# A three-pass transformer block on one core: one gate product fewer, another order of the drain of the second pass, and a weight sum ahead of the keys

## The chip, the core and the metric

The kernel runs on one core of a Trainium2 chip. A core has TensorE (matmuls, PE in the profile; its weight loads are PEld), VectorE (DVE), ScalarE (ACT), GpSimd (POOL) and SyncE (SP), which here only issues DMAs. Each engine takes its own list of instructions in order; engines wait for each other and for DMAs on semaphores. Matmuls read SBUF and write PSUM, and another engine has to empty PSUM. The metric is the device time of one execution in microseconds; lower is better. The time of a kernel is the median of several runs.

## The reference, cut to what matters

Inputs are 4 x 1024 tokens of 1024 numbers, in float32. The block is "macaron" shaped: half a feed-forward, attention, and half of the same feed-forward again.

```python
def ffn(x):                        # weight (1024,1024), centroids (64,1024)
    dots = softmax(x @ centroids.T / 0.1)
    hits = dots > 0.01
    query_sel = any(hits, axis=1)  # one flag per token
    cluster_sel = any(hits, axis=0)            # one flag per cluster, over ALL tokens
    row_sel = cluster_sel[assignments]         # one flag per output column
    dense = x @ weight.T + bias
    return where(query_sel[:, None] & row_sel[None, :], dense, 0)

def attn(x):                       # 32 query heads of 32, 8 key/value heads
    q, k, v = x @ Wq + bq, x @ Wk + bk, x @ Wv + bv
    scores = einsum('bsdh,bseh->bsde', q, k) / sqrt(32)    # 32 x 32 for every token
    return einsum('bsde,bseh->bsdh', softmax(scores), v)

x = x + 0.5 * ffn(layernorm(x))
x = x + attn(layernorm(x))
x = x + 0.5 * ffn(layernorm(x))
```

The attention mixes within one token, so there is no dependence between tokens there. The feed-forward has one: `cluster_sel` needs the gate of every token before the first output can be masked.

## The kernel before

The tokens are 32 tiles of 128. Because of `cluster_sel` there are three passes. The first makes the dense product and the gate of the first feed-forward. The second adds it, does the attention, and makes the gate (and the last 256 dense columns) of the second feed-forward. The third makes the remaining dense product, adds, and stores the result.

Everything stands in an order written by hand: the tile framework's manual schedule keeps the instructions on each engine's list as the Python code issues them, and derives only the semaphores. Generators are used for this: `next(steps)`, `next(two)`, `next(sums)` issue the next piece of a longer computation at that place of the list.

Products of two tiles with the 768 first columns are made by Strassen's method in Winograd's form: `winograd` (L258) makes seven products of quarter size in place of eight, numbered 1, 5, 2, 6, 7, 3, 4 in the order of issue. It needs four sums of activations s1 to s4 (`token_sums`, L242) and four sums of weights t1 to t4 (`weight_sums`, L233); both run on GpSimd. t1 uses the weight blocks w12 and w11; t2 uses w22 and t1; t3 uses w22 and w12; t4 uses w21 and t2. `project_two` (L785) is the same for the projection to queries, keys and values, with sums `qsums` of the projection's weights, which are kept in the place of the feed-forward's weight blocks during the second pass. The feed-forward's blocks wait in DRAM (`wtd`) and are loaded again (`returns`, L985) before the drain; the sums t1 to t4 then take the place of the projection's weights.

The second pass is the loop at L990 over s = 0 to 36. Step s is a software pipeline: it projects tile s, makes the keys of s-1 (`keys`, GpSimd, L857), scores and softmax of b = s-2 (`scores`, `weighted`, `attend`: matmuls `sc` at L880, VectorE's maximum L889 and subtraction L891, ScalarE's exp L1000, VectorE's transpose `stt` L900, matmuls `po` L922, four VectorE steps L932/L934 to `o`), the residual add of g = s-3 (`second_added`, GpSimd, L946), its layernorm (`moments` on VectorE with the square root on ScalarE, `normed` on ScalarE), the transposes of f = s-4 (`transposed`, matmuls `tp` L205 and ScalarE copies L206), and the gate products of a = s-5 or f (`gate_2`, L974: `ffn_part`, eight matmuls of 320 columns, then VectorE's evacuation L222, maximum L388, subtraction L391, ScalarE's exp L397 and VectorE's bookkeeping L403 to L409 in `gates_used`). `scores` and `attend` use the same PSUM buffer (tag `att`, one buffer).

The projected tile goes to DRAM and back to be regrouped (`rearranged`, L844: one load `qk`, four loads `v`), and so does the attention's result (`od`, `ot`). All these DMAs stand on SP's queue, in program order; the stores of `store_2` (L966) and of y stand on GpSimd's.

From s = 32 on, nothing is projected any more: this is the drain. Its TensorE cover is the dense product of the last six tiles (26 to 31, called kept), by `winograd` over pairs. Its weight sums are issued at L1102 to L1104 (the first ahead of s1, the second by the `between` of `token_sums`, L253, between s2 and s3) and at L1067 to L1069. The gate product of tile 27 is issued at s = 31 (L1113, as f) and, because `gates_used` has emptied `es` by then, once more at s = 32 (L1114, as a).

Of the kernel before, what the change touches and what calls it, by code (L numbers as in the profile page):

```python
# [42 lines left out]
def kernel(  # L43
# [39 lines left out]
    nc = tc.nc  # L83
    xf = x.flatten_outer_dims()
    of = out.flatten_outer_dims()
    NT = xf.shape[0] // P
# [48 lines left out]
    xt, dt_, xT = {}, {}, {}  # L135
# [40 lines left out]
    def normed(src, mv, name):  # L176

        sc = scales(mv, name)
        xn = row(f"xn_{name}")
        nc.scalar.activation(xn, src, AF.Identity, bias=sc[:, 1:2], scale=sc[:, 0:1])  # L180
        return xn
# [16 lines left out]
    def transposed(xn, name):  # L198

        t_ = row(f"xT_{name}").rearrange("p (k c) -> p k c", c=P)  # L200
        for h in range(2):
            tp = bank(f"tp_{name}_{h}").rearrange("p (j c) -> p j c", j=4)
            for j in range(4):
                k = 4 * h + j
                nc.tensor.transpose(tp[:, j, :], xn[:, k * P : (k + 1) * P], ident)  # L205
            nc.scalar.copy(t_[:, 4 * h : 4 * h + 4, :], tp)  # L206
        return t_
# [31 lines left out]
            engine.tensor_tensor(o, p, q, ALU.subtract)  # L239
            yield  # L240

    def token_sums(xT, a, b, name, between=lambda: None):  # L242

        a11, a12, a21, a22 = xT[a][:, :4], xT[a][:, 4:], xT[b][:, :4], xT[b][:, 4:]
        ss = []
        for i in range(2):
            r = row(f"ts{i}_{name}_{a}").rearrange("p (h k c) -> p h k c", h=2, k=4)
            ss += [r[:, 0], r[:, 1]]
        s1, s2, s3, s4 = ss
        sub = ALU.subtract  # L250
        nc.gpsimd.tensor_tensor(s1, a21, a22, ALU.add)  # L251
        nc.gpsimd.tensor_tensor(s2, s1, a11, sub)
        between()  # L253
        nc.gpsimd.tensor_tensor(s3, a11, a21, sub)
        nc.gpsimd.tensor_tensor(s4, a12, s2, sub)
        return ss

    def winograd(a, b, ss, ts, pool, name, held=False):  # L258
# [206 lines left out]
    with (  # L465
# [214 lines left out]
        for t in range(3, NT):  # L680
# [17 lines left out]
            if t % 2 == 1:  # L698
                a = t - 3
# [66 lines left out]
    with (  # L766
# [90 lines left out]
        def keys(qk, t):  # L857

            kd = attn.tile([P, NBLK, 4, D], F32, tag="kd", name=f"kd{t}")
            nc.gpsimd.tensor_tensor(  # L860
                kd,
                qk[:, :, D:].unsqueeze(2).to_broadcast([P, NBLK, 4, D]),
                tmask.unsqueeze(1).unsqueeze(3).to_broadcast([P, NBLK, 4, D]),
                ALU.mult,
            )
            return kd
# [79 lines left out]
        def second_added(ot, rs, t):  # L946
            nc.gpsimd.tensor_tensor(ot, ot, rs.unsqueeze(1).to_broadcast([P, HKV, D]), ALU.mult)

            xv = xt[t].rearrange("p (d g r) -> p d g r", g=HKV, r=REP)
            ov = ot.rearrange("p g d -> p d g").unsqueeze(3).to_broadcast([P, D, HKV, REP])  # L950
            nc.gpsimd.tensor_tensor(xv, xv, ov, ALU.add)  # L951
# [7 lines left out]
        def has(t):  # L959
            return 0 <= t < NT  # L960
# [24 lines left out]
        def returns(*some):  # L985

            for i in some:
                nc.sync.dma_start(out=blocks(wc)[i], in_=wtd[i])

        for s in range(NT + 5):  # L990
            b, g, f, a = s - 2, s - 3, s - 4, s - 5
            paired, odd = s in PAIRED, s % 2 == 1
            if has(s + 4):
                load_2(s + 4)
            if s == NT - 1:
                returns(1, 0)
            if has(b):
                sc = scores(qkv[b][0], kd.pop(b), b)
            if has(b):
                nc.scalar.activation(sc, sc, AF.Exp, scale=QK_SCALE)  # L1000
            if paired:
                if not odd:
                    two = project_two(s, s + 1, ss2)
                next(two)
            if has(s + 1) and s + 1 not in xT2:
                xT2[s + 1] = transposed(xn2.pop(s + 1), f"2_{s + 1}")
            if has(s - 1):
                kd[s - 1] = keys(qkv[s - 1][0], s - 1)
            if has(g):
                second_added(ot.pop(g), rs.pop(g), g)  # L1010
            if g >= 0 and g < FIRST_KEPT:
                nc.gpsimd.dma_start(out=y2[g], in_=xt[g])
            if odd or not paired:
                gates_used()
            if 3 <= s <= 4:
                next(qsums)
            if has(s + 2):
                normal = sums_normed(xt[s + 2], f"2_{s + 2}")
                next(normal)
            if paired and not odd:  # L1020
                next(two)
            if NT <= s < NT + 2:

                next(steps)
            if has(b):
                st, rs[b] = weighted(sc, b, lambda: next(two) if paired and odd else None)
            if s == NT - 1:
                returns(3, 2)
            if paired and not odd:
                if has(s + 3):  # L1030
                    first_added(s + 3)
                next(two)
            if has(s + 2):
                xn2[s + 2] = next(normal)
            if paired and not odd:
                next(two)
            if paired and odd:
                gate_2(a)
                xT[f] = transposed(xn3.pop(f), f"3_{f}")
            if paired and not odd:  # L1040
                fo = attend(st, qkv.pop(b)[1], b)
            if s == NT + 2:
                dt_[a] = row(f"d3_{a}")
                steps = winograd(s - 6, s - 5, ss, ts, None, 3)
                for _ in range(3):
                    next(steps)
            for _ in range({NT: 3, NT + 1: 1}.get(s, 0)):
                next(steps)
            if has(g):
                mv = moments(xt[g], f"3_{g}")  # L1050

            def between():
                if has(s + 3) and s + 3 in dt_:
                    first_added(s + 3)
                if has(g):
                    xn3[g] = normed(xt[g], mv, f"3_{g}")

            if paired:
                if not odd:
                    next(two)  # L1060
                between()
            elif has(s):
                flat[s] = project(xT2.pop(s), s, between)
            else:
                between()
                k = s - NT
                if k == 0:  # L1067
                    for _ in range(2):
                        next(sums)  # L1069
                if k == 1:  # L1070
                    next(steps)
                if k > 2:
                    load_xT(k - 3)
                if 2 <= k < 4:
                    for _ in range(1 if k == 2 else 3):
                        next(steps)
            if paired and odd:
                qkv[s] = rearranged(flat.pop(s), s)
            if has(b) and b in qkv:
                fo = attend(st, qkv.pop(b)[1], b)  # L1080
            if s in flat:
                qkv[s] = rearranged(flat.pop(s), s)
            if has(b):
                ot[b] = returned(fo, b)
            if has(s - 1):
                qkv[s - 1] = (qkv[s - 1][0], values(qkv[s - 1][1], s - 1))
            if has(f) and f in xn3:
                xT[f] = transposed(xn3.pop(f), f"3_{f}")
            if odd and s + 1 in PAIRED:
                xT2[s + 2] = transposed(xn2.pop(s + 2), f"2_{s + 2}")  # L1090
                ss2 = token_sums(xT2, s + 1, s + 2, "2q")
            if 1 <= s <= 3:

                for _ in range(2 if s == 1 else 1):
                    next(held[s // 2])
                i = {1: NT - 4, 3: NT - 2}.get(s)
                for i in (i, i + 1) if i else ():
                    nc.sync.dma_start(out=d1[i], in_=dt_.pop(i))
            if s == 1:
                next(qsums)  # L1100
            if s == NT - 1:
                sums = weight_sums(blocks(wc), ts, [nc.gpsimd] * 4)  # L1102
                next(sums)
                ss = token_sums(xT, f - 1, f, 2, lambda: next(sums))  # L1104
                steps = winograd(f - 1, f, ss, ts, None, 3)
            if s == NT + 1:
                ss = token_sums(xT, f - 1, f, 2)
                asg = load_assigned()
            if s == NT + 3:
                hot = one_hot(asg)  # L1110
            if paired:
                if odd:
                    gate_2(f)  # L1113
            elif has(a) and a not in es:  # L1114
                gate_2(a)
            for i in sorted(es) if odd or not paired else ():
                es[i] = gate_exp(es[i], i, 1)


# [116 lines left out]
```

## Time and profile before

| | us |
|---|---|
| median of three runs (lowest, highest) | 1315.55 (1314.51, 1317.08) |
| the profiled execution | 1315.4 |
| its span, first to last instruction | 1313.7 |
| TensorE busy in the span | 1299.6 |
| VectorE, GpSimd, ScalarE busy | 881.3, 602.0, 493.9 |
| gate products, `ff`, all 720 records | 201.5 |
| second pass, first projection by pairs (s = 4) | from 497.1 |
| drain, first `winograd` product of tile 26 | from 987.3 |
| first product of the last pair, tile 30 | 1053.6 |

A row of the timeline reads: start, duration, engine, source line, operation, the tile written and the tiles read, shape, count; in brackets the idle time of the engine just before and what released it. An fp32 matmul has two records, so a gate product has 16. A row of a stretch reads: its length, the busy time of TensorE, its weight loads, VectorE, ScalarE and GpSimd (with the number of instructions), then the granted TensorE clock as a share of full speed, the mean busy share of the DMA engines, and GB/s.

### The profile page before, as it was taken

Reading aid. Unit: us, or ns where it says so; the run is one execution under the profiler, and the core shown is the slowest. Engines: PE = TensorE matmul, PEld = TensorE weight load, DVE = VectorE, ACT = ScalarE, POOL = GpSimd, SP = SyncE. Lnnn points to the kernel's source line nnn. Section 1 sums busy time; section 2 is a strip of 40 time slices with the busy share of each in tenths; the row PEclk is TensorE's granted clock in tenths of the full one; section 3 lists DMA queues with packets and bytes.
Section 4 is the critical chain, followed back from the end, with each engine's and each line's share of the span. In section 5 each row is a group of like instructions: output and inputs, shape, how many; then the busy total and the mean of one; then the engine's idle time right before and its main releaser. Section 6 shows DMA issues by size and latency. Waiting matters only on the chain.

```text
span 1313.7 us, 22704 instructions
## 1 busy us (share of the span) xinstructions
PE 1299.6 (99%) x8726; PEld 842.1 (64%) x8726; DVE 881.3 (67%) x1800; ACT 493.9 (38%) x823; POOL 602.0 (46%) x460
## 2 busy tenths in 40 slices
PE   8999999999999999999999999999999999999998
PEld 7665777777776665666666666666666655555554
DVE  4565557656546367888888888888878348555556
ACT  4433322332211346666666667666644200000000
POOL 3622113312113347567666666666557326633440
PEclk9999999999999999999999999999999999999999
DMA  8866877776215256456666666656443346665522
GB/s 295 146 168 127 189 157 165 159 197 119 65 56 193 68 157 183 142 179 198 193 189 198 201 185 201 186 181 201 121 119 97 104 148 237 223 208 178 178 109 81
DMA packets 283332, 213.45 MB, mean 162 GB/s; under 512 B 227608, under 2 KB 242200, under 8 KB 283224
## 3 DMA queue, kind: packets, MB, share of 16 engines
q1 hardware_dynamic: 265596, 163.99, 46.0%
q0 software_dynamic: 8736, 30.68, 6.3%
q10 hardware_dynamic: 8892, 17.33, 3.6%
q8 instruction: 69, 1.13, 0.4%
q14 instruction: 39, 0.32, 0.1%
HBM read 127.77 MB, written 84.18 MB: 161 GB/s over the span
## 4 chain that ended last, share of the span: by engine, by line
PE 94%; POOL 2%; DVE 2%; DMA 1%; issue 0%; ACT 0%; POOLq 0%; SPq 0%; ACTq 0%
PE st L279 42%; PE qs L804 20%; PE ff L212 14%; PE la L343 6%; PE tp L205 4%; PE pq L212 2%; PE sc L880 2%; PE po L922 2%; POOL wqkv L239 1%; PE tpw L554 0%; DMA qkvd<-qkv 0%; POOL x L951 0%; DVE bn L162 0%; DMA x<-in_L_attn_x_dram 0%; DMA qk<-qkvd 0%
## 5 line engine op out<-in xcount | busy, mean ns | idle before, releaser
L251 POOL TENSOR_TENSOR ts<-xT 128x512 f32<-128x512 f32 x32 | 41.8, 1306 | 360.3 <-DVE sc L171 166.9
L270 DVE TENSOR_TENSOR d<-st,d 128x384 f32<-128x384 f32 x162 | 89.2, 552 | 170.5 <-PE st L279 169.3
L212 PE MATMUL ff<-wc,xT 128*128 128x320 f32 x720 | 201.5, 433 | 1.4 <-ACT xT L206 0.6
L279 PE MATMUL st<-wc,xT 128*128 128x384 f32 x512 | 175.9, 487 | 0.0
L212 PEld LDWEIGHTS ff<-wc,xT 128*128 128x128 f32 x720 | 135.0, 190 | 57.2 <-ACT xT L206 1.2
L279 PEld LDWEIGHTS st<-wc,xT 128*128 128x128 f32 x512 | 96.0, 190 | 62.0 <-issue 0.6
L860 POOL TENSOR_TENSOR kd<-qk,tmask 128x1024 f32<-128x1024 f32 x32 | 60.6, 1894 | 155.5 <-DMA qk<-qkvd 155.5
L279 PE MATMUL st<-ws,ts 128*128 128x384 f32 x384 | 131.2, 487 | 0.0
L279 PE MATMUL st<-wqkv,ts 128*128 128x384 f32 x384 | 129.6, 487 | 0.0
L804 PE MATMUL qs<-wc,ts_2q 128*128 128x384 f32 x336 | 114.4, 491 | 0.0
L447 DVE SCALAR_TENSOR_TENSOR d<-d,qsel,mask 128x1024 f32<-128x1024 f32 (+2 forms) x68 | 108.4, 1594 | 0.2
L279 PEld LDWEIGHTS st<-wqkv,ts 128*128 128x128 f32 x384 | 72.9, 190 | 51.1 <-issue 1.0
L458 POOL TENSOR_TENSOR x<-x,d 128x1024 f32<-128x1024 f32 x32 | 75.4, 2357 | 61.4 <-DVE d L447 47.2
L165 ACT ACTIVATE mv<-mv,eps 128x1 f32<-128x1 f32 x66 | 19.4, 295 | 217.0 <-DVE mv L164 212.4
L270 DVE TENSOR_TENSOR d<-st,brow 128x384 f32<-128x384 f32 x96 | 52.8, 550 | 70.7 <-PE st L279 70.6
L279 PEld LDWEIGHTS st<-ws,ts 128*128 128x128 f32 x384 | 71.3, 190 | 42.9 <-issue 0.8
L804 PEld LDWEIGHTS qs<-wc,ts_2q 128*128 128x128 f32 x336 | 62.7, 190 | 43.5 <-issue 2.8
L162 DVE BATCH_NORM_STATS2 bn<-x 128x6 f32<-128x512 f32 x132 | 84.3, 680 | 5.8 <-DMA x<-in_L_attn_x_dram 4.3
L279 PE MATMUL st<-wc,ts 128*128 128x384 f32 x256 | 87.8, 486 | 0.0
L206 ACT COPY xT<-tp 128x512 f32<-128x512 f32 x138 | 73.1, 580 | 30.8 <-PE tp L205 30.8
L804 PE MATMUL qs<-wqkv,xT 128*128 128x384 f32 x224 | 80.0, 501 | 0.0
L951 POOL TENSOR_TENSOR x<-x,ot 128x1024 f32<-128x1024 f32 x32 | 76.1, 2378 | 2.5
(143 smaller groups left out, 2253.7 us busy)
## 6 DMA issues: line engine op xcount, KB each, us to landing
x<-in_L_attn_x_dram SPq DMA_DIRECT2D x64, 512.0 KB
d<-d SPq DMA_DIRECT2D x64, 512.0 KB
out_dram<-x ACTq DMA_DIRECT2D x30, 512.0 KB
xb<-in_L_attn_x_dram SPq DMA_DIRECT2D x108, 128.0 KB
y<-x POOLq DMA_DIRECT2D x26, 512.0 KB, 3.2
xTd<-xT POOLq DMA_DIRECT2D x26, 512.0 KB, 6.0
xT<-xTd SPq DMA_DIRECT2D x26, 512.0 KB
x<-y SPq DMA_DIRECT2D x26, 512.0 KB
```

The lines of the kernel that those rows point to most:

```text
L162: nc.vector.bn_stats(st[:, i, :], src[:, i * 512 : (i + 1) * 512])
L205: nc.tensor.transpose(tp[:, j, :], xn[:, k * P : (k + 1) * P], ident)
L206: nc.scalar.copy(t_[:, 4 * h : 4 * h + 4, :], tp)
L212: nc.tensor.matmul(p, src[:, k, :], wts[:, k, lo:hi], start=(k == 0), stop=(k == KT - 1))
L270: nc.vector.tensor_tensor(out, ps, other, ALU.add)
L279: nc.tensor.matmul(ps, src[:, k, :], wts[:, k, :], start=(k == 0 and onto is None), stop=(k == 3), skip_group_check=onto is not None,)
L343: nc.tensor.matmul(ps, src[:, k, :], wts[:, k, :], start=(k == 0 and onto is None), stop=(k == 3), skip_group_check=onto is not None,)
L447: nc.vector.scalar_tensor_tensor(d[:, sl], d[:, sl], qsel[which][:, t : t + 1], mask[:, sl], ALU.mult, ALU.mult)
L458: nc.gpsimd.tensor_tensor(xt[t], xt[t], dt_.pop(t), ALU.add)
L804: nc.tensor.matmul(ps, src[:, k, :], wts[:, k, :], start=(k == 0 and onto is None), stop=(k == 3), skip_group_check=onto is not None,)
L860: nc.gpsimd.tensor_tensor(kd, qk[:, :, D:].unsqueeze(2).to_broadcast([P, NBLK, 4, D]), tmask.unsqueeze(1).unsqueeze(3).to_broadcast([P, NB ...
L951: nc.gpsimd.tensor_tensor(xv, xv, ov, ALU.add)
```

## The change

It has three parts, all in the second pass.

First, the gate product of tile 27 is issued once (`elif has(a) and s > NT + 1`). Since it now lies in `es` until s = 33, `gates_used` and `gate_exp` are left out at s = 32, and the bookkeeping of tiles 26 and 27 is done at s = 33.

Second, the steps s = 32 and s = 33 are put in another order. At s = 32: GpSimd's t2 stands after s1 and s2 of the pair 26/27 as before, but the keys of tile 31 come next, then s3 and s4 (kept back in `late`), t3, the residual add of 29, and t4. The moments and the normalisation of tile 29 move from s = 32 to s = 33, behind the scores of 31. At s = 33: product 7 of the pair 26/27 stands ahead of the scores of 31, the products 3 and 4 after them, then `attend` of 31, then the gate product of tile 28 (before: after the transposes of 29), then the moments and normalisation of tile 30 (before: ahead of `attend`), and the transposes of 29. On SP's queue the loads of the blocks w22 and w21 (`returns(3, 2)`) move from before the `qk` and `v` loads of tile 31 to behind them.

Third, the third of the `qsums` is issued at s = 3 ahead of the keys of tile 2, not behind the residual add and store of tile 0.

```diff
-    def token_sums(xT, a, b, name, between=lambda: None):
+    def token_sums(xT, a, b, name, late=None):
...
         nc.gpsimd.tensor_tensor(s1, a21, a22, ALU.add)
         nc.gpsimd.tensor_tensor(s2, s1, a11, sub)
-        between()
-        nc.gpsimd.tensor_tensor(s3, a11, a21, sub)
-        nc.gpsimd.tensor_tensor(s4, a12, s2, sub)
+
+        def others():
+            nc.gpsimd.tensor_tensor(s3, a11, a21, sub)
+            nc.gpsimd.tensor_tensor(s4, a12, s2, sub)
+
+        if late is None:
+            others()
+        else:
+            late.append(others)
         return ss
...
             if s == NT - 1:
                 returns(1, 0)
+            if s == NT + 1:
+                next(steps)
             if has(b):
                 sc = scores(qkv[b][0], kd.pop(b), b)
...
+            if s == 3:
+                next(qsums)
+            if s == NT:
+                next(sums)
             if has(s - 1):
                 kd[s - 1] = keys(qkv[s - 1][0], s - 1)
+            if s == NT:
+                late.pop()()
+                next(sums)
             if has(g):
                 second_added(ot.pop(g), rs.pop(g), g)
+            if s == NT:
+                next(sums)
             if g >= 0 and g < FIRST_KEPT:
                 nc.gpsimd.dma_start(out=y2[g], in_=xt[g])
-            if odd or not paired:
+            if (odd or not paired) and s != NT:
                 gates_used()
-            if 3 <= s <= 4:
+            if s == 4:
                 next(qsums)
...
-            if NT <= s < NT + 2:
+            if s == NT:
 
                 next(steps)
+            if s == NT + 1:
+                xn3[f] = normed(xt[f], moments(xt[f], f"3_{f}"), f"3_{f}")
             if has(b):
                 st, rs[b] = weighted(sc, b, lambda: next(two) if paired and odd else None)
-            if s == NT - 1:
-                returns(3, 2)
...
-            for _ in range({NT: 3, NT + 1: 1}.get(s, 0)):
+            for _ in range({NT: 3, NT + 1: 2}.get(s, 0)):
                 next(steps)
-            if has(g):
+            if NT <= s < NT + 2:
+                fo = attend(st, qkv.pop(b)[1], b)
+            if s == NT + 1:
+                gate_2(a)
+            if has(g) and s != NT:
                 mv = moments(xt[g], f"3_{g}")
 
             def between():
                 if has(s + 3) and s + 3 in dt_:
                     first_added(s + 3)
-                if has(g):
+                if has(g) and s != NT:
                     xn3[g] = normed(xt[g], mv, f"3_{g}")
...
                 between()
                 k = s - NT
-                if k == 0:
-                    for _ in range(2):
-                        next(sums)
-                if k == 1:
-                    next(steps)
...
             if paired and odd:
                 qkv[s] = rearranged(flat.pop(s), s)
+            if s == NT - 1:
+                returns(3, 2)
...
                 next(sums)
-                ss = token_sums(xT, f - 1, f, 2, lambda: next(sums))
+                late = []
+                ss = token_sums(xT, f - 1, f, 2, late)
...
-            elif has(a) and a not in es:
+            elif has(a) and s > NT + 1:
                 gate_2(a)
-            for i in sorted(es) if odd or not paired else ():
+            for i in sorted(es) if (odd or not paired) and s != NT else ():
                 es[i] = gate_exp(es[i], i, 1)
```

## The prediction

> **What bounds the kernel now.** I read the page's shares first, then the chain of waits, then TensorE's timeline for gaps, and last the timelines of the other engines around each gap.
>
> ```profile
> PE 1299.6 (99%) x8726; PEld 842.1 (64%) x8726; DVE 881.3 (67%) x1800; ACT 493.9 (38%) x823; POOL 602.0 (46%) x460
> PE 94%; POOL 2%; DVE 2%; DMA 1%; issue 0%; ACT 0%; POOLq 0%; SPq 0%; ACTq 0%
> ```
>
> TensorE sets the end: 1299.6 of 1313.7 us busy. A product taken out is worth its time, unless the engines that worked behind it become visible. Only two places matter here, the start of the second pass and its drain. At the start (columns: start, us, engine; the last line is a stretch, with the granted clock third from the end):
>
> ```profile
> 482.51 1.89 POOL L860 TENSOR_TENSOR kd<-qk,tmask 128x1024 f32<-128x1024 f32 x1 [7.31 <-DMA qk<-qkvd]
> 488.57 3.46 POOL L239 TENSOR_TENSOR wc<-wqkv 128x1536 f32<-128x1536 f32 x1
> 489.43 3.69 DVE L447 SCALAR_TENSOR_TENSOR d<-d,qsel,mask 128x1024 f32<-128x1024 f32 x1
> 494.33 1.52 DVE L934 SCALAR_TENSOR_TENSOR o<-po,tmask,o 128x256 f32<-128x256 f32 x3
> 496.11 1.06 PE L880 MATMUL sc<-kd,qk 32*32 32x128 f32 x64 [1.88 <-DMA qkvd<-qkv]
> 497.10 4.54 PE L804 MATMUL qs<-wqkv,xT 128*128 128x384 f32 x8
> 497.00:501.00 4.00, 4.00 (x22) 2.15 (x8) 2.45 (x2) 1.31 (x3) 3.80 (x4) 0.57 0.70 128
> ```
>
> L447 takes 1.27 us elsewhere (at 440.17, 471.49) and 3.69 here: it ends 1.1 after GpSimd's weight sum, which began first. That makes L934 end at 495.85, and the scores, which reuse its PSUM tile, start 0.26 later. (The DMA that the row names is a later one on the same semaphore.) The gap is followed by a granted clock of 0.57 over four us.
>
> The drain:
>
> ```profile
> 977.80 1.71 SPq L988 DMA_DIRECT2D wc<-wtd x2
> 984.43 0.38 SPq L848 DMA_DIRECT2D qk<-qkvd x1
> 984.86 6.67 SPq L854 DMA_DIRECT2D v<-qkvd x4
> 985.00:991.00 6.00, 6.00 (x82) 3.58 (x81) 5.22 (x12) 2.95 (x6) 5.92 (x4) 1.00 1.05 399
> 994.00:997.00 3.00, 3.00 (x11) 1.81 (x10) 2.97 (x5) 0.00 (x0) 3.00 (x3) 1.00 0.17 53
> 989.50 3.44 POOL L239 TENSOR_TENSOR wqkv<-wc,wqkv 128x1536 f32<-128x1536 f32 x1
> 990.26 2.76 DVE L409 SCALAR_TENSOR_TENSOR best<-ge,gsm,best 128x64 f32<-128x64 f32 x1
> 999.82 4.47 PE L212 MATMUL ff<-wc,xT 128*128 128x320 f32 x16
> 1004.92 1.06 PE L880 MATMUL sc<-kd,qk 32*32 32x128 f32 x64 [0.63 <-DVE o L934]
> 1031.91 4.57 PE L212 MATMUL ff<-wc,xT 128*128 128x320 f32 x16 [0.46 <-DVE d L270]
> ```
>
> The product at 999.82 is the second one of tile 27. TensorE waits for only 1.1 us in all between 987 and 1060, so the order there is tight; DMA is full until 991 (share 1.05, 399 GB/s) and idle after 994.
>
> All times below are on the clock of this execution (1315.4 us, span 1313.7 and 1.7 around it; the median of the runs, 1315.55, is 0.15 more).
>
> **The front: weight sum before the keys.** The third query sum writes a block of wc that a product of tile 30 reads until 477.3. GpSimd then idles until 482.51, so the 3.46 us fit in the 7.31 of idling and cost nothing; without that cover the keys would be 3.46 later. L447 then runs in 1.27 instead of 3.69: 2.4 earlier, so L934 ends at 493.4 and, with 0.26, the scores could start at 493.7. TensorE is through with the product before at 494.2, so the 1.88 go. The eight matmuls at 497.10 took 4.38 to the next group (501.48) against 2.68 for the same eight at 929.77: 1.7 of slow clock, which I expect to go too. The token sums that follow come 2.4 earlier as well (they wait for a ScalarE copy, behind an activation that waits for VectorE behind L447), at 493.4 to 496.0, and are wanted at 497.9. Sum: -3.6; bounds 0 (L447 still blocked) and -3.6. After that the steady part shows no gap over 0.7, so the 3.6 is kept until the drain.
>
> What the trace shows of the clock is a gap of 1.88 and one us of 32-wide matmuls, then 3.4 us at half speed. The Trainium skill, TensorE: Matmul & The Clock Gate, "Why this matters for your kernels", allows gaps up to about 3 us; by it the front would give 1.9 only, and of the drain's new gaps below the two longest alone would cost clock. I go by the row.
>
> **The drain, what leaves.** One gate product, 16 records, 4.31 us on the chain; seven small VectorE steps (1.7 us), a table load and an exp on ScalarE, none on the path. The 1.1 of old waits go too: -5.4. But those 4.31 us were also cover.
>
> **The drain, what is added,** with durations from the rows and the changed kernel's order on each engine.
>
> (1) The loads of w22 and w21 (L988, 768 KB each) move on SP's queue behind the qk and v loads of tile 31. The qk load cannot go before 984.43 (it waits for its store); four v issues take 2.0 to 2.5 when the queue is not full (937.36, 972.80); so the loads go out near 987.3 instead of 977.8. Outstanding then: GpSimd's four stores issued 981.2 to 983.4 (1.3 MB), qk and v (0.4 MB), the two loads (1.6 MB): 3.3 MB at 399 GB/s is 8.3 from 985.3, and 1.4 for v's small packets: w21 lands near 995, w22 2.2 before. Bounds: as today (w22 by 989.4, when the sum starts unhindered, w21 by 992.5, when its product starts) and 2.5 later than I take. TensorE reaches the product with w21 at 992.59: +2.5. GpSimd's sum t2 (w22 in it) starts at 992.9 instead of 989.50. The keys of tile 31 are now behind it, but their scores come late enough.
>
> (2) GpSimd then has keys 1.89, two token sums 2.5, t3 3.45: t3 at 1004.1. The changed order has the product with t3 before the scores of 31; TensorE, with the 4.31 gone, stands there at 1002.3: +1.85. For t4 likewise (0.72 + 2.36 + 3.45 later): +0.35.
>
> (3) The scores of 31 start at 1006.8. On VectorE the maximum (1.23) and subtraction (1.22) end at 1010.4. Then, now ahead of the transpose stt that the product po of 31 waits for, come the gate bookkeeping of 26 and 27 (1.1) and the moments of 29 (1.5), whose square root ScalarE takes 0.4 and VectorE uses in 0.5. The second L409 meets GpSimd's residual add of 30 (2.35, 1011.4 to 1013.7) and is held as at 990.26: +2.1. stt (1.25) ends at 1017.2, po could start at 1013.3: +4.1; without the hold +2.0.
>
> (4) The gate product of 28 now stands before the transposes of 29 and ends at 1022.7; transposes 1.0 and one product 2.6 follow, then s1 of 28 and 29 is wanted, at 1026.3. But ScalarE's copies of that transpose stand behind the normalisation of 30, which waits for moments that VectorE makes after evacuating the gate product: 0.2 + 0.9 + 1.5 + 0.4 + 0.5 to 1026.05, normalisation 1.24, copies 1.2, s1 1.27: 1029.9. +3.6. Before, the copies came 1.7 after the transposes began (1014.85, 1016.51) and the sum was covered by the gate product.
>
> (5) The gate product of 29 needs a PSUM bank that VectorE empties behind the moments of 31, which wait for GpSimd's add of 31 (behind the sums just delayed): +1.85, 0.46 before.
>
> Added waits: 2.5 + 1.85 + 0.35 + 4.1 + 3.6 + 1.85 = 14.2; less 5.4: +8.8. Bounds: with the loads as today (1) is 0 and (2) 1.1, so +4.6, and without the hold in (3) +2.5; with the loads 2.5 later +11.3. (6) Clock: gaps of 4.1 and 3.6 are longer than the 1.88 that cost 1.7. The first slows the gate product that everything in (4) hangs on, the second is half absorbed by (5): +2 of a possible 0 to 4.
>
> Sum: -3.6 + 8.8 + 2 = +7.2 on 1315.4; I take 0.5 off for small waits that overlap: **1322 us**.
>
> **Rivals.** Slower by 0.2% needs 2.6 us, which is about what a measurement of this kernel can tell.
>
> (a) Faster: VectorE's new order does not hold TensorE. Its place is (3) and (4), worth 7.7 and the 2 of clock: 1322 - 9.7 = 1312. It decides from 9.3 us saved on. For it: the copies of 29 could overlap if the normalisation of 30 were early. Against: ScalarE and VectorE run in order, and the gate product stands before the moments. Chance 0.10.
>
> (b) No difference: the loads land as today and neither hold nor clock comes: -3.6 + 2.5 = 1314.3; with the hold 1316.4. For it: SP's queue is free when the loads are issued. Against: full DMA until 991. Chance 0.13.
>
> (c) The front does not do what it says, because another GpSimd step meets L447: 1322 + 3.6 = 1326. GpSimd has none ready at 489.4. Chance 0.07.
>
> **How the numbers follow.** Forecast 0.70, (c) 0.07: slower 0.77; (b) same 0.13; faster 0.10. The forecast's own range is 1318 (loads as today) to 1327 (loads 2.5 later, more clock); with (b) taken in, 1315 to 1327.
>
> **What would show it.** Right: L447 near 1.3 at 489, no gap at 494 and clock 1.00 after it; TensorE gaps ahead of the product with w21, ahead of po of 31 (released by stt) and ahead of the second product of 28 (released by the token sum), 3 to 4 us each. Wrong: gaps under 1 us at the last two, or a drain (987 to the first product of the last pair at 1053.6) that is shorter than today's 66 us.

## The result and the profile after

| | before | after |
|---|---|---|
| median of the runs, us (lowest, highest) | 1315.03 (1312.86, 1317.08; 4 runs) | 1323.02 (1322.62, 1324.02; 4 runs) |
| span of the profiled execution | 1313.7 | 1320.6 |
| drain begins (first product of the pair 26) | 987.32 | 983.95 |
| first product of the last pair, tile 30 | 1053.55 | 1060.49 |
| drain, the difference of the two | 66.23 | 76.54 |

The ratio is 1.0063 (95% interval 1.005 to 1.0077): slower. Timed again later, on the chip of the second set of experiments, it was 1.0049 (1.0037 to 1.0061): 1320.98 against 1313.74. Between the two traces, the start of the pass gives 3.4 us, the drain takes 10.3, and the rest is equal (260.1 us from the last pair's first product to the end in both).

What TensorE waited for in the changed kernel (waiting engine and line, releaser, then us in total, times, longest):

```profile
PE po L928 <- DVE stt L906: 3.8, 1, 3.8
PE st L285 <- POOL ts L251: 3.3, 1, 3.3
PE st L285 <- DMA wc<-wtd: 2.7, 1, 2.7
...
PE st L285 <- POOL wqkv L239: 1.4, 1, 1.4
```

All four are new, and all four lie in the drain. TensorE's timeline there, the rows that a wait precedes and the gate product of 28 (start, us, engine, line):

```profile
992.11 2.85 PE L285 MATMUL st<-wc,xT 128*128 128x384 f32 x8 [2.73 <-DMA wc<-wtd]
...
1000.91 2.85 PE L285 MATMUL st<-wqkv,ts 128*128 128x384 f32 x8 [1.35 <-POOL wqkv L239]
...
1014.09 1.51 PE L928 MATMUL po<-stt,vt 32*32 32x128 f32 x64 [3.81 <-DVE stt L906]
1015.53 5.55 PE L212 MATMUL ff<-wc,xT 128*128 128x320 f32 x16
...
1027.88 4.47 PE L285 MATMUL st<-wqkv,ts 128*128 128x384 f32 x8 [3.34 <-POOL ts L251]
...
1038.85 4.57 PE L212 MATMUL ff<-wc,xT 128*128 128x320 f32 x16 [0.46 <-DVE d L276]
```

Read the durations too. `po` takes 1.51 instead of 1.07, the gate product 5.55 instead of 4.47, the product behind the fourth wait 4.47 instead of 2.74. The stretches around them say why (length, busy time of TensorE, its weight loads, VectorE, ScalarE, GpSimd, then the granted clock, the DMA share and GB/s):

```profile
1010.00:1014.00 4.00, 0.28 (x1) 0.00 (x0) 3.57 (x8) 1.41 (x2) 0.49 (x1) 1.00 0.00 0
1014.00:1015.50 1.50, 1.41 (x64) 0.97 (x64) 1.43 (x3) 0.13 (x1) 0.00 (x0) 0.54 0.00 0
1015.50:1021.00 5.50, 5.50 (x24) 3.80 (x18) 2.89 (x7) 0.00 (x0) 0.00 (x0) 0.81 0.16 27
...
1028.00:1032.00 4.00, 4.00 (x8) 2.24 (x9) 1.50 (x5) 1.43 (x3) 4.00 (x4) 0.60 0.17 61
```

In the first stretch TensorE works 0.28 of 4 us while VectorE is nearly full; then the clock is at about half. From start to start, `po` lost 0.44, the gate product 1.08 and the third one 1.72: 3.2 us of clock.

At the front the masked product (L447 before, L453 now) and the scores behind it:

```profile
489.31 1.28 DVE L453 SCALAR_TENSOR_TENSOR d<-d,qsel,mask 128x1024 f32<-128x1024 f32 x1
494.47 1.07 PE L886 MATMUL sc<-kd,qk 32*32 32x128 f32 x64
```

1.28 instead of 3.69, and no bracket ahead of the scores: nothing is waited for.

### The profile page after: what moved, and what is told of

It is laid out like the page before. It is cut to its first block, busy times and chain, and to the rows that moved or that the text cites. A ratio compares the mean times of both kernels' runs of the same rounds, so it can differ in the third digit from the quotient of the medians.

```text
span 1320.6 us, 22656 instructions
## 1 busy us (share of the span) xinstructions
PE 1299.0 (98%) x8710; PEld 840.3 (64%) x8710; DVE 873.7 (66%) x1793; ACT 491.2 (37%) x819; POOL 605.6 (46%) x460
## 4 chain that ended last, share of the span: by engine, by line
PE 95%; DVE 2%; POOL 1%; DMA 1%; ACT 0%; issue 0%; SPq 0%; ACTq 0%; POOLq 0%
PE st L285 42%; PE qs L810 20%; PE ff L212 14%; PE la L349 6%; PE tp L205 5%; PE pq L212 3%; PE sc L886 2%; PE po L928 2%; POOL wqkv L239 1%; DMA wc<-wtd 1%; PE tpw L560 1%; DVE bn L162 0%; DMA x<-in_L_attn_x_dram 0%; PE pm L447 0%; DVE best L415 0%
## 5 line engine op out<-in xcount | busy, mean ns | idle before, releaser
L212 PE MATMUL ff<-wc,xT 128*128 128x320 f32 x704 | 198.3, 435 | 1.0 <-ACT xT L206 0.6
L453 DVE SCALAR_TENSOR_TENSOR d<-d,qsel,mask 128x1024 f32<-128x1024 f32 (+2 forms) x68 | 102.8, 1512 | 0.2
L464 POOL TENSOR_TENSOR x<-x,d 128x1024 f32<-128x1024 f32 x32 | 75.5, 2360 | 59.8 <-DVE d L453 32.1
L162 DVE BATCH_NORM_STATS2 bn<-x 128x6 f32<-128x512 f32 x132 | 84.3, 680 | 4.5 <-DMA x<-in_L_attn_x_dram 4.2
```

The source lines that it names most:

```text
L162: nc.vector.bn_stats(st[:, i, :], src[:, i * 512 : (i + 1) * 512])
L212: nc.tensor.matmul(p, src[:, k, :], wts[:, k, lo:hi], start=(k == 0), stop=(k == KT - 1))
L453: nc.vector.scalar_tensor_tensor(d[:, sl], d[:, sl], qsel[which][:, t : t + 1], mask[:, sl], ALU.mult, ALU.mult)
L464: nc.gpsimd.tensor_tensor(xt[t], xt[t], dt_.pop(t), ALU.add)
```

## The experiments

There were eleven runs, on nine new kernels and once more on each of the two known ones. Those that are compared by their times ran beside the kernel before, in three sets, each on one chip: the front alone, the gate product alone, the loads back and the softmax ahead with a median of before of 1313.49; the normalisation of 30, the changed kernel again and all causes undone with 1313.74; the last three with 1314.38. Across sets the ratios to before are the fairer comparison. Where a median hides a cause, the drain of the profiled execution (as in the table above) is given.

**The front alone.** The kernel before with the third part of the change.

```diff
+            if s == 3:
+                next(qsums)
             if has(s - 1):
                 kd[s - 1] = keys(qkv[s - 1][0], s - 1)
...
-            if 3 <= s <= 4:
+            if s == 4:
                 next(qsums)
```

> The kernel before with the third part of the change alone (third query sum ahead of the keys of tile 2). Theory (the sum held VectorE's masked product; nothing else in the second pass absorbs the gain): no gap at 494, no slow clock behind it, the drain as before; span 1313.7 - 3.5 = 1310.2, median about 1311.5 against 1315.0, ratio 0.997. Rival (what is gained at the front is given back at a later wait of the pass): 1314 to 1316.

Measured: 1312.60 against 1313.49, ratio 0.9992 (0.9983 to 1.0002). The trace at the front is as the theory says (no wait, no slow clock), but the gain is 0.9 and its interval takes in none: neither theory's number. One new wait stands in its drain, 0.43 ahead of the product with w21, so a little is given back, as the rival has it. Either more of it is given back, or the profile before was no typical one. Hence:

**The kernel before, once more.**

> The kernel before, unchanged, looked at once more. The front alone gave 0.9 us, not 3.5, and the profile of the run with the single gate product, whose front is that of before, shows a gap of 0.76 at 494 and no slow clock. Theory (when GpSimd's weight sum starts against VectorE's masked product differs between executions, and the profile that the prediction used is one of the long ones): the masked product takes 2 to 3 us here and the gap at 494 is under 1.2 us, without slow clock, span 1310.5 to 1312.5; or it is again 1.88 with slow clock and 1313.7. Rival (the gap is always 1.88, and the run with the single product differed for a reason of its own): 1.88 and 1313.7. A single look can only refute the rival, not confirm it.

Its GpSimd and VectorE rows, and the scores of the same place:

```profile
487.70 3.45 POOL L239 TENSOR_TENSOR wc<-wqkv 128x1536 f32<-128x1536 f32 x1
489.36 2.89 DVE L447 SCALAR_TENSOR_TENSOR d<-d,qsel,mask 128x1024 f32<-128x1024 f32 x1
495.24 1.06 PE L880 MATMUL sc<-kd,qk 32*32 32x128 f32 x64 [0.66 <-DMA qkvd<-qkv]
```

The same program waits 0.66 here and 1.88 in the profile that was predicted from; the rival falls. With the two experiments below that keep the old front there are four executions of it:

| execution | keys of 2 begin | weight sum begins | masked product takes | gap ahead of the scores | slow clock | drain begins |
|---|---|---|---|---|---|---|
| before, again | 481.25 | 487.70 | 2.89 | 0.66 | none | 984.71 |
| before, single product | 481.26 | 487.71 | 2.99 | 0.76 | none | 984.76 |
| before, as predicted from | 482.51 | 488.57 | 3.69 | 1.88 | 3.41 | 987.32 |
| joined order, old front | 484.03 | 490.09 | 3.69 | 3.00 | 3.41 | 988.65 |

The keys wait for the load of qk (released by that DMA in all four), and the weight sum follows 6.1 to 6.5 us behind them. The nine executions with the new front begin the drain at 983.56 to 984.41. So the new front begins the drain 0.3 to 5 us earlier, by when one DMA lands in the old one.

**The gate product alone.** The kernel before without its second product of the gate of 27, nothing moved.

```diff
-            elif has(a) and a not in es:
+            elif has(a) and s > NT:
                 gate_2(a)
```

> The kernel before with the second product of the gate of tile 27 left out and nothing else moved. Theory (the 4.31 us were cover for o of tile 30, whose steps on VectorE stand behind the moments of 29, which wait for GpSimd's residual add): TensorE stands some 5.3 us ahead of the scores of 31, released by o on VectorE, in place of the product and of 0.63 of waiting; the first product of the last pair stays at 1053.6; a gap as long as this may cost up to 1.7 of slow clock: 1315 to 1317. Rival (the product lies on the path and its time is saved, as a list of TensorE's work would have it): 1310.7.

Measured: 1315.72 against 1313.49, ratio 1.0011 (0.9998 to 1.0023). The theory, with a wait of 4.8 for 5.3: the product gone, no time won. Its timeline, TensorE, VectorE and GpSimd:

```profile
995.57 2.36 POOL L951 TENSOR_TENSOR x<-x,ot 128x1024 f32<-128x1024 f32 x1
...
997.97 1.28 DVE L162 BATCH_NORM_STATS2 bn<-x 128x6 f32<-128x512 f32 x2 [0.68 <-POOL x L951]
...
1000.70 1.52 DVE L934 SCALAR_TENSOR_TENSOR o<-po,tmask,o 128x256 f32<-128x256 f32 x3
1002.48 1.32 PE L880 MATMUL sc<-kd,qk 32*32 32x128 f32 x64 [4.82 <-DVE o L934]
1003.73 4.02 PE L279 MATMUL st<-wqkv,ts 128*128 128x384 f32 x8
```

Read upwards: the scores of 31 stand 4.82 us for o of tile 30; o stands on VectorE behind the moments of 29 (L162), which stood for GpSimd's residual add. The 4.31 were all cover, and the new gap brings slow clock (4.02 for 2.85). The drain is 67.8 long, 1.6 longer than with the product; by the times the difference from before is not clear of noise.

**The loads back.** The changed kernel with `returns(3, 2)` where it was before.

> The changed kernel with the loads of w22 and w21 back ahead of the qk and v loads of tile 31, nothing else. Theory (the late loads cost the wait ahead of the product with w21, and a part of it comes back one step later because the weight sum t3 is wanted earlier than it is made): the wait of 2.73 goes to about 0.3, the one ahead of product 7 grows from 1.35 to about 1.9, the waits for stt and for the token sum stay near 3.8 and 3.3: 1323.0 - 2.4 = 1320.6. Rival A (both waits are the loads'): -4.1, 1318.9. Rival B (the scores and keys of 31 are late for another reason, so all is given back ahead of po): 1323.

Measured: 1320.92 against 1313.49, ratio 1.0051 (1.0037 to 1.0065). The waits are the theory's: none ahead of the product with w21, 1.69 ahead of product 7, 3.80 for stt, 3.34 for the token sum; 2.4 less of waiting. But in the profiled execution the slow clock behind `po` lasted 6.83 us instead of 3.41, and the drain is 75.5, 1.1 shorter. By the medians the part cannot be told from nothing beside the second timing of the changed kernel (1.0049), whose drain is 75.0. Rival A is out, since the wait ahead of product 7 stays. The price of the loads comes from a cleaner place, below.

**The softmax ahead of the bookkeeping.**

```diff
-            if s == NT + 1:
-                xn3[f] = normed(xt[f], moments(xt[f], f"3_{f}"), f"3_{f}")
             if has(b):
                 st, rs[b] = weighted(sc, b, lambda: next(two) if paired and odd else None)
+            if s == NT + 1:
+                gates_used()
+                xn3[f] = normed(xt[f], moments(xt[f], f"3_{f}"), f"3_{f}")
```

(`gates_used` no longer stands in its first place at s = 33.)

> The changed kernel with the transpose stt of tile 31 (and the softmax sum) ahead of the gate bookkeeping of 26 and 27 and of the moments and normalisation of 29, at s = 33. Theory (the order on VectorE makes the wait ahead of po): that wait of 3.8 goes under 0.5 and with it the slow clock behind it (1.5); the moments of 29 come later, so the transposes of 29 or the token sum behind them are waited for by some 2 us more: 1323.0 - 1.8 - 1.5 = 1319.7. Rival (the softmax of 31 itself, sc to exp, sets po, and VectorE's other steps fit beside it): 1323.

Measured: 1319.61 against 1313.49, ratio 1.0041 (1.0029 to 1.0054); drain 73.0, 3.5 shorter than in the changed kernel's first profile and 1.9 shorter than in its second. The intervals of the ratios overlap, so the trace has to carry the reading. The wait for stt is gone (the transposes of 29 wait 0.49 in its place) and the one behind it has grown from 3.34 to 4.48, as the theory has it: a part of what is saved comes back there. VectorE of the changed kernel shows what stood ahead of stt:

```profile
1008.50 2.08 DVE L415 SCALAR_TENSOR_TENSOR best<-ge,gsm,best 128x64 f32<-128x64 f32 x1
1010.50 1.27 DVE L162 BATCH_NORM_STATS2 bn<-x 128x6 f32<-128x512 f32 x2
...
1012.71 1.23 DVE L906 STREAM_TRANSPOSE stt<-s 128x1024 f32<-128x1024 f32 x1
```

L415 is held until GpSimd's residual add of 30 (1008.14 to 1010.49) ends: 2.08, against 0.27 in the experiment, where that add was not under way. stt could have started behind the exp, which ended at 1008.44.

**The normalisation of 30 behind the transposes of 29**, and the changed kernel beside it.

```diff
-            if has(g) and s != NT:
+            if has(g) and not NT <= s < NT + 2:
                 mv = moments(xt[g], f"3_{g}")
...
             if has(f) and f in xn3:
                 xT[f] = transposed(xn3.pop(f), f"3_{f}")
+            if s == NT + 1:
+                xn3[g] = normed(xt[g], moments(xt[g], f"3_{g}"), f"3_{g}")
```

> The changed kernel with the moments and the normalisation of tile 30 behind the transposes of 29 and their copies, at s = 33 and later, nothing else. Theory (ScalarE's place of the copies behind the normalisation of 30 makes the wait ahead of the second product of 28): that wait of 3.34 goes, with the slow clock behind it (about 1.7); the gate product of 29 then waits some 1.5 in place of 0.46; the wait for stt stays 3.8: the changed kernel - 4, near 1319 where that is at 1323. Rival (the residual add of 30 on GpSimd, ahead of the token sums, makes the wait): no difference.

> The changed kernel, unchanged, timed beside the kernel before on the chip of these runs. Front 0.9 saved, drain 10.3 added by its trace: before + 9.4. Rival (the front saves 3.5): before + 6.9. Waits as in its first profile (2.7, 1.35, 3.8, 3.3, 0.46); how much slow clock follows the two long ones differs between executions, 3 to 6 us.

Measured: 1318.51 (1315.43 to 1320.17) with the edit and 1320.98 (1317.92 to 1322.85) without, against 1313.74; ratios 1.0032 (1.002 to 1.0044) and 1.0049. 2.5 less, not the 4 that the theory gave, and the rival's nothing is not excluded by the times. The trace decides: no wait for the token sum at all, and 1.27 ahead of the gate product of 29 in place of 0.46. ScalarE and GpSimd of the changed kernel (its first profile):

```profile
1024.28 1.24 ACT L180 ACTIVATE xn<-x,sc 128x1024 f32<-128x1024 f32 x1 [0.53 <-DVE sc L173]
1025.43 1.05 ACT L206 COPY xT<-tp 128x512 f32<-128x512 f32 x2
1026.56 1.26 POOL L251 TENSOR_TENSOR ts<-xT 128x512 f32<-128x512 f32 x1 [16.07 <-ACT xT L206]
```

The transposes were done at 1021.96, the copies came 3.5 later, behind the normalisation; GpSimd had been idle for 16 us, so its residual add was not what held it. The edit's execution had 3.79 and 4.16 of waiting at the other two places and 10.2 us of slow clock, so its drain is 74.1, only 0.9 below that of the changed kernel's second profile (75.0). That one differs from its own first one: 3.35 for w21, then 6.83 of slow clock, under which the wait for t3 vanished and the one for stt fell to 1.99. A late step slows what follows, and the slower stretch hides the next wait; the terms of the sum do not simply add. The changed kernel stands 7.2 above before here, nearer to the rival's 6.9 than to the theory's 9.4. But its drain is shorter here too: between the second profiles of the two kernels the drain takes 8.6 (75.0 against 66.4) and the front gives 1.15.

**All causes undone** (below: the joined order). The changed kernel with the loads back; t2, s3, s4, t3 ahead of the keys of 31 on GpSimd, t4 behind them and the residual add of 29 last; stt ahead of the moments of 29; the bookkeeping of the gates behind o of 31 (26, 27) and, at s = 34, behind the evacuations (28); moments and normalisation of 30 and 31 behind the transposes of the tile before. (The lines show where the steps stand now; they no longer stand in their old places.)

```diff
             if s == NT:
                 next(sums)
+                late.pop()()
+                next(sums)
             if has(s - 1):
                 kd[s - 1] = keys(qkv[s - 1][0], s - 1)
             if s == NT:
-                late.pop()()
                 next(sums)
             if has(g):
                 second_added(ot.pop(g), rs.pop(g), g)
-            if s == NT:
-                next(sums)
...
-            if s == NT + 1:
-                xn3[f] = normed(xt[f], moments(xt[f], f"3_{f}"), f"3_{f}")
             if has(b):
                 st, rs[b] = weighted(sc, b, lambda: next(two) if paired and odd else None)
+            if s == NT + 1:
+                xn3[f] = normed(xt[f], moments(xt[f], f"3_{f}"), f"3_{f}")
+            if s == NT - 1:
+                returns(3, 2)
...
             if s == NT + 1:
+                gates_used()
                 gate_2(a)
...
             if has(f) and f in xn3:
                 xT[f] = transposed(xn3.pop(f), f"3_{f}")
+            if has(g) and s > NT:
+                xn3[g] = normed(xt[g], moments(xt[g], f"3_{g}"), f"3_{g}")
...
+            if s == NT + 2:
+                gates_used()
             if paired:
```

> The single gate product and the front, with all the found causes undone: loads of w22 and w21 ahead of qk and v; t2, s3, s4, t3 ahead of the keys of 31, t4 behind them, residual add of 29 last; stt of 31 ahead of the moments of 29; gate bookkeeping of 26 and 27 behind o of 31, that of 28 behind the evacuations of the pair 28; moments and normalisation of 30 and 31 behind the transposes of the tile before. Theory (each wait has its own cause and none is needed by the arithmetic): no wait over 0.8 between 985 and 1050, the drain is 5.3 shorter than before's 66.2, and with 0.9 of the front 1313.5 - 6.2 = 1307.3, ratio 0.995. Rival (the drain is bound by VectorE, GpSimd and the DMAs together, so that waits come back elsewhere): 1312 to 1316.

Measured: 1307.39 (1307.09 to 1308.17) against 1313.74, ratio 0.9953 (0.994 to 0.9965): faster than both kernels. The drain is 61.3, 4.95 shorter than the first profile of before. What TensorE waits for in it (the head of the list):

```profile
PE tp L205 <- ACT xn L180: 2.3, 1, 2.3
PE warm L531 <- POOL tq L106: 1.5, 1, 1.5
PE tpw L560 <- DMA wn<-in_L_ffn_weight_dram: 0.7, 1, 0.7
PE qs L810 <- DVE qkv L843: 0.7, 1, 0.7
PE ff L212 <- ACT xT L206: 0.6, 2, 0.3
```

None of these lies in the drain. The products of the drain where the changed kernel waits:

```profile
989.04 2.85 PE L285 MATMUL st<-wc,xT 128*128 128x384 f32 x8
...
1005.36 1.07 PE L928 MATMUL po<-stt,vt 32*32 32x128 f32 x64
...
1014.23 2.74 PE L285 MATMUL st<-wqkv,ts 128*128 128x384 f32 x8
...
1023.37 4.57 PE L212 MATMUL ff<-wc,xT 128*128 128x320 f32 x16 [0.37 <-DVE d L276]
```

Three without a bracket, one with 0.37. The same single product, the same order on TensorE; only the order on the other engines and on SP's queue differs.

**Three steps away from the joined order.** First, the gate product of 27 a second time:

```diff
-            elif has(a) and s > NT + 1:
+            elif has(a) and s != NT + 1:
                 gate_2(a)
```

(The exp of that second product is taken at s = 32.)

> The joined order (1307.4) with the gate product of 27 put back a second time at s = 32, behind the transposes of 28. Theory (in this order nothing is waited for there, so the product is no cover but work on the path): 4.3 us slower, 1311.7. Rival (what the single product gives is small in any order, and the joined order gains elsewhere): 1308 or less.

Measured: 1311.69, 4.3 above the joined order; the drain is 66.2 against 61.3, the 4.31 and 0.48 of waiting for w21 in that execution. By the ratios (0.9972, 0.9963 to 0.9982, against 0.9953) the step is 2.5, since the kernel before was timed 0.6 higher beside this one and its own times spread; the rival's 1308 is out. A product that was worth nothing in the old order is worth 2.5 to 4.3 by the times in this one, and in the trace its full 4.31.

Second, the old front in the joined order (the first diff above, undone).

> The joined order with the third query sum back behind the residual add and store of tile 0. Theory (the gap at 494 is 0.7 in most executions and 1.9 with slow clock in some): median 0.7 to 1.0 slower, 1308.1 to 1308.4, with some executions near 1310.5 to 1311. Rival (the front is worth the 3.5 of the first profile): 1310.9 as the median.

Measured: 1309.82 (1307.73 to 1312.05), 2.4 above the joined order, ratio 0.9964 (0.9951 to 0.9977), by which the step is 1.4 and not clear of noise. Both figures lie between the theory's 0.7 to 1.0 and the rival's 3.5. The runs spread over 4.3 us where the joined order spreads over 1.1. It fits the table of four executions, not one number: what the new front buys is 0.9 in one comparison, 1.4 to 2.4 in the other, and there less spread too.

Third, the loads late in the joined order.

> The joined order with the loads of w22 and w21 behind the qk and v loads of tile 31, as the change has them. Theory (the late block is waited for by the third product and nothing later gives it back): a gap of 2.7 to 3.8 ahead of the product with w21 and up to 3.4 of slow clock behind it: 1310 to 1314, 1311.5 taken. Rival (the slack of the joined order takes the late loads in): 1307.4 to 1308.

Measured: 1310.73 (1310.31 to 1311.93), ratio 0.9968 (0.9956 to 0.9981): 3.3 above the joined order by the medians, 2.0 by the ratios, whose intervals overlap. The drain is 65.9, 4.6 longer. Its one new row:

```profile
992.15 4.37 PE L285 MATMUL st<-wc,xT 128*128 128x384 f32 x8 [2.76 <-DMA wc<-wtd]
```

2.76 of waiting, and 4.37 for what takes 2.85 at full clock. Together that is 4.3 of the 4.6: what moving `returns(3, 2)` costs in this execution, with no other wait near it.

## Why the prediction was right, point by point

**Front, -3.6.** The mechanism is shown (L453 at 1.28, no gap, full clock), and the trace gains 3.4. The size was misjudged: it was the gain against one execution, taken as that of the kernel. Alone it gave 0.9, in the joined order 1.4 to 2.4. The row it was read from was also less singular than "1.27 us elsewhere" says: in the same trace the masked product takes 2.65 at 451.36 (under the keys) and 2.27 at 505.04 (under the residual add), without a wait of TensorE over 0.7 near them. What counted at 489 was that the scores needed what stood behind it. The forecast in absolute time held because it was built on that same execution (1315.4, while the medians of before in the later runs are 1313.5 to 1314.4); by medians side by side the change costs 7 to 8 us, and the drain more than all of it.

**Cover, -5.4.** "Those 4.31 us were also cover" was the right sentence to write, and was too weak: with only the product out, nothing at all was gained.

**(1) +2.5:** 2.73 measured, 2.4 to 3.8 in the other executions with late loads. For the 1.4 of v's small packets in its working no row is given; the sum held, since the product began at 992.11 in a drain that began 3.4 earlier, which is 995.5 on the clock of before. **(2) +1.85 and +0.35:** 1.35 and none. With the loads early it was 1.69, so this wait is the order's own and not the loads'. It is gone in the joined order; no run changed GpSimd's order alone. **(3) +4.1:** 3.81, with the second bookkeeping step held by the residual add as foreseen (2.08); gone when stt stands first. **(4) +3.6:** 3.34, by the copies behind the normalisation of 30; gone when they stand first.

**(5) +1.85:** 0.46, as before. This term failed, and the clock hid it: TensorE came 1.72 late through the product ahead, so VectorE waited for TensorE until 1034.96, and GpSimd's add of 31, which should have held the moments, had ended at 1034.72. In the execution where (4) had been taken out, and its slow clock with it, the moments of 31 did wait 0.71 for that add, and the gate product 1.27. **(6) +2 of clock:** 3.2, two stretches of 3.41 us at half clock.

The drain's sum was 8.8 + 2 - 0.5 = 10.3, and 10.3 was measured: the waits came out 2.5 too large (11.7 for 14.2), the clock 1.2 too small, 0.8 had no term (part of it is the 0.16 by which matmul groups overlap in the profile where nothing waits between them), and the 0.5 taken off for overlap was not needed. Such a close sum is partly luck, as the second execution shows (75.0 instead of 76.5, other waits).

The lower bound does not follow from its own terms: 14.2 less 2.5 for (1), 1.1 for (2) and the 5.4 is 5.2, not 4.6, so the range would have begun near 1318.5 and rival (b) near 1315. With the loads back (2) was 1.69, not 1.1. Of the three gaps of "3 to 4 us each" the one for w21 was shorter, 2.73. And the row for 994 to 997 shows a DMA share of 0.17, which is little but not idle.

None of the rivals came: the changed kernel's VectorE order did hold TensorE, the loads did land late, and no other step met the masked product.

## What to carry to other kernels

Before a piece of work is taken off the bounding engine, ask what the others finish behind it: here the same 4.31 us product was worth nothing in one order and 2.5 to 4.3 in another, and the order on VectorE, ScalarE and GpSimd made the difference. When steps are moved, put the one that the bounding engine waits for (transpose, copies, evacuations) ahead of bookkeeping and of normalisations that are wanted later, on every engine's own list. And price a stall from more than one execution when a DMA sets its start.

## What the runs showed of the hardware

**Slow clock behind gaps.** Over all drains and fronts profiled here, each of the eleven gaps of 3.00 to 4.82 us of TensorE came with half clock, for 3.41 or 6.83 us, which began between 1.9 us before the gap's end and 1.3 us after it. Of five shorter ones two did (1.88, 2.76) and three did not (1.99, 2.38, 2.73); none of 1.7 and below did. So a shorter gap is a matter of chance, seen from the program: the wait for w21 was 2.73 at full clock in one execution, and in another 2.76 with 1.5 of clock behind it.

The Trainium skill, TensorE: Matmul & The Clock Gate, "Why this matters for your kernels", asks to avoid idle gaps over about 3 us. Above 3 the rows here agree without exception; below, two of five show that it is no safe bound.

**Held VectorE steps.** Two steps of VectorE with two inputs in SBUF end shortly after a GpSimd step under which they start, the masked product 1.1 us after it and the 64-wide bookkeeping step 0.1. The masked product takes 1.28 alone and 2.89 to 3.69 under the weight sum, the bookkeeping step 0.27 alone and 2.08 under the residual add. How long a step is held depends on when the GpSimd step starts, which here hung on a DMA.
